# Attention values through DRAM by tokens, and the last layer's normalised input transposed by DMA

## The chip, the cores and the metric

The kernel runs on one core of a Trainium2 chip. The metric is the device time of one execution in microseconds (us). The core has five instruction streams that matter here: TensorE (PE in the profile, with its weight loads as PEld), VectorE (DVE), ScalarE (ACT), GpSimd (POOL) and SyncE (SP). SP computes nothing: every transfer of this kernel is issued from its one queue, in order, and an instruction that waits holds everything behind it.

## The reference

Input: `x` and `ctx`, each 32 batches of 128 tokens (rows) by 1024 columns. Two layers, each an attention and a feed-forward part with a residual, run over every batch independently:

```
x = x + L0_xattn(layernorm(x), ctx, ctx)   # autocorrelation by FFT, top 9 of 128 lags
x = x + L0_ffn(layernorm(x), ...)          # x @ W_base.T + mixture of 8 low-rank experts, 2 chosen
x = x + L1_xattn(layernorm(x), ctx, ...)   # attention in a window of 16
x = x + L1_ffn(layernorm(x), A, B, Wr)     # mixture of 4 low-rank experts, 2 chosen
```

The change is in the last two. In `L1_xattn` the 128 rows are channels (8 heads of 16) and the 1024 columns are the sequence:

```
q = Wq @ x + bq;  k = Wk @ ctx + bk;  v = Wv @ ctx + bv       # 128x128 by 128x1024
k, v padded with zeros: 8 columns on the left, 7 on the right
dots[h, t, w] = sum_d q[h, d, t] * k[h, d, t + w] / 4          # w = 0..15
out[h, d, t]  = sum_w softmax_w(dots)[h, t, w] * v[h, d, t + w]
x = x + Wo @ out + bo
```

In `L1_ffn` each of the 128 rows is a token of 1024 features: `logits = x @ Wr.T` (4 experts), the two largest pass a softmax, `mid = x @ A.T` (64 columns in all), each expert's 16 columns are multiplied by its gate, and the result is multiplied by `B`.

## The kernel before

**Layout.** A batch is held as two halves `g` of 128 x 512 (f32). Matrix products that need more than half precision are made of fp16 pairs: a number is split into a high and a low fp16 part (`split`), and `three` adds the products high*high, high*low, low*high in one accumulation in PSUM.

**Order.** `mk_kernel` does not emit instructions as it records them. A `Planner` notes every operation with the tiles it touches, and `plan` runs a list scheduler over the whole program: it gives every operation an estimated duration (`_cost`), a priority (batch number, length of the chain behind it, a bias by stage from `CFG`) and a tile slot, and puts it into its engine's order. `emit` then issues all of them in that order, so the order on each engine is fixed when the kernel runs, several batches are in work at a time, and every instruction comes from one line (L363 in the profile). Groups are therefore known by their tiles: `u` is one of 43 buffers of 128 x 512 f32, `d` one of 2 of twice that size, `p` a PSUM bank, `s`, `t`, `m`, `r` small tiles. `CFG` holds two phases of scheduling parameters, the second from 1459.1 on, with one bias for each stage, and a factor 1.013 on the durations of ACT, DVE and POOL.

**Stages of a batch**: `load`, `spec`, `corr`, `top`, `wt`, `inv` (layer 0's attention, for each half), `ffn0`, `gate`, `base` (its feed-forward part), then `kv`, `q`, `S`, `PV`, `wo` (layer 1's attention) and `ffn1`.

**Values before** (`attention`, L820). For each half, `three` makes `p = Wv @ ctx` (weights `wv16`, three matmuls of 512 columns), ACT adds the bias and scales it into a `u` tile, and `split` with `eng=G` makes the pair: ACT writes the high part and POOL the low part into `vpad`, a constant of 128 x 1040 x 2 fp16 whose 8 columns at each end stay zero. The product `PV` needs values by token, not by channel. So DVE transposes `vpad` in 32 x 32 blocks of 32-bit words (a word is the pair) into `d` tiles, four times a batch (L847), and SP copies them into `vbd`, a block-diagonal weight tensor of one half (128 x 32 blocks x 128 x 2 fp16), by four transfers for each half (L874). `vbd` is one buffer: the four transfers of a half can go only when the products of the half before have read it. The queries go into `qbd` in the same manner, by eight transfers for each half (L871). `S` and `PV` then run 96 matmuls of 32 columns each for a half, 48 for each quarter `qt`.

**Layer 1's feed-forward input before** (`ffn1`, L918). `ln` takes the sums of the residual, ACT squares the two halves for the variance, POOL takes the power -0.5, and `normalise` (ACT) writes the normalised half `xn`. `transposed` (L773) turns it by four TensorE transposes of 128 x 128 into a PSUM bank, ACT writes the high part from there (with the scale 32*1024) and DVE the low part (`t16`). Twelve matmuls of 68 columns for each half, with `t16` as weights and `ar4` as the moving operand, give the experts' middle columns and the logits. `ffn0` and `wt` use TensorE transposes too; they stay.

Of the kernel before, what the change touches and what calls it, by code (L numbers as in the profile page):

```python
# [14 lines left out]
F16 = mybir.dt.float16  # L15
# [12 lines left out]
TINY = 1e-30  # L28
CFG = {'nu': 43, 'nd': 2, 'en': 'G', 'cl': 'G', 'xl': 'G', 'sm': 'V', 'sw': 'A', 'wg': 'VG', 'q0': 'G', 'ns': 28, 'nt': 48, 'plan': {'phases': [{'at': 0.0, 'T': 19.88, 'margin': 178, 'win': 5, 'su': 60, 'sp': 3, 'ru': 1, 'rp': 0, 'bias': {'kv': -5.1, 'load': 10.0, 'S': -6.7, 'gate': 38.6, 'ffn1': 7.4, 'q': 0.4, 'top': 1.3, 'PV': -5.6, 'inv': 3.4, 'wt': 4.5, 'spec': 5.4, 'wo': 41.4, 'ws': -9.4, 'base': -1.7, 'ffn0': 90.1, 'corr': 5.4, 'setup': -12.6}}, {'at': 1459.1, 'T': 30.14, 'margin': 69, 'win': 6, 'su': 57, 'sp': 1, 'ru': 2, 'rp': 1, 'bias': {'kv': -32.9, 'load': -45.0, 'S': 18.4, 'gate': 125.0, 'ffn1': -67.8, 'q': 29.1, 'top': -23.6, 'PV': -37.2, 'inv': 57.1, 'wt': -20.7, 'spec': -56.0, 'wo': -29.3, 'ws': -71.2, 'base': -21.0, 'ffn0': 60.9, 'corr': -125.0, 'setup': 2.0}}], 'slack': [1.013, 0, 0]}}
NTOP = int(2 * math.log(S))  # L30
# [10 lines left out]
class _View:  # L41
# [26 lines left out]

    def windows(self, n, step, width):
        return self._step("__getitem__", (slice(None), slice(0, 1)))._wrap(n, step, width)  # L70

    def _wrap(self, n, step, width):
        f = lambda ap: bass.AP(ap.tensor, ap.offset, [list(ap.ap[0]), [step, n], [1, width]])
        return _View(self.tile, f(self.proto), self.path + ((f, None, None),))

    def resolve(self):
# [3 lines left out]
        return ap  # L80

    def region(self):

        ap = self.proto
        size = mybir.dt.size(ap.dtype)
        dims = [list(d) for d in ap.ap]
        row = dims[0][0]
        p0, f0 = divmod(ap.offset, row)
        last = f0 + sum(s * (n - 1) for s, n in dims[1:])
        return p0, p0 + dims[0][1], f0 * size, (last + 1) * size  # L90


class _Tile:
    def __init__(self, cls, slot=None, const=False):
        self.cls, self.slot, self.const = cls, slot, const
        self.log, self.users = [], {}

# [8 lines left out]
class Planner:  # L106
# [72 lines left out]
    def _cost(self, op, method, v, kw):  # L179
# [27 lines left out]
        elif eng == "DVE":  # L207
            n = max(n, size(src))
            two = method in ("tensor_copy", "tensor_scalar", "memset") and not psum and n > 64
            op.dur += 6 * n / 0.96 + 67 if method == "reciprocal" else (n * (0.5 if two else 1.0) + 64 + 59 * nsc) / 0.96  # L210
            op.dur += 70.0 * ("accum_out" in v) + {"match_replace": 67.0, "transpose": 25.0}.get(method, 0.0)
        elif eng == "Pool":
            small = mybir.dt.size(out.proto.dtype) == 2
            if method == "memset":
                op.dur += 40.0 + (0.85 if small else 0.2) * n
            else:
                rate = (2.8 if small else 1.2) if method == "tensor_scalar" else 1.88 if small else 2.1
                if any(x.proto.ap[-1][0] == 0 for x in v.values()) and n > 128:
                    rate = 1.67
                op.dur += 530.0 if kw.get("op") == ALU.pow else 150.0 + rate * n  # L220
        else:
            run = out.proto.ap[-1][1] * mybir.dt.size(out.proto.dtype)
            dram = any(x.tile is None for x in v.values())
            op.dur += (3200.0 if dram else 2900.0 if run > 128 else 3500.0) + out.shape[0] * n * mybir.dt.size(out.proto.dtype) / 360.0

            op.cold = 450.0 if dram else 720.0 if run > 128 else 840.0


# [5 lines left out]
    def plan(self, phases, slack):  # L234
# [45 lines left out]
        while events:  # L280
            now = events[0][0]
            if phases and now >= phases[0][0]:
                period, window, margin, scarce, reserve, bias = phases.pop(0)[1]
                prio = lambda o: (period * max(o.batch, 0) - o.tail - bias.get(o.stage, 0.0), o.index)
                ready = {e: sorted((prio(o), o) for _, o in l) for e, l in ready.items()}
# [80 lines left out]
def plan_args(c):  # L366
    us = lambda v: v * 1e3
    scarce = lambda f: {"u": f["su"], "p": f["sp"], "d": 9, "m": 3, "r": 9, "s": 9, "t": 9}
    reserve = lambda f: {"u": f["ru"], "p": f["rp"], "m": 1, "s": 4, "t": 6}
# [5 lines left out]
def mk_kernel(ctx: ExitStack, tc: tile.TileContext, T: dict, out: bass.AP):  # L375
# [4 lines left out]
    cp = ctx.enter_context(tc.tile_pool(name="const", bufs=1))  # L380
    pp = ctx.enter_context(tc.tile_pool(name="psum", bufs=1, space=PSUM))

    def slot(name, shape, dt=F32):
# [3 lines left out]
        "u": [slot(f"u{i}", [128, HALF]) for i in range(CFG["nu"])],  # L387
        "d": [slot(f"d{i}", [128, D]) for i in range(CFG["nd"])],
        "p": [pp.tile([128, HALF], F32, tag=f"p{i}", name=f"p{i}") for i in range(8)],
# [27 lines left out]
    def const(name, shape, dt=F32):  # L417
        return P.fixed(slot(name, shape, dt), const=True)

    def load(name, shape=None, dt=F32):  # L420
# [40 lines left out]
    k16 = keep("k16", [128, 2, D + 16], F16, 0.0)  # L461
    vpad = keep("vpad", [128, D + 16, 2], F16, 0.0)

# [19 lines left out]
    pb = B()  # L483
    PE.matmul(pb[:, 0:3], lhsT=blk1, rhs=bsum, start=True, stop=True)
    bqs, sq, bqsc, uq = (const(n, [128, 1]) for n in ("bqs", "sq", "bqsc", "uq"))
    V.tensor_scalar(bqs, pb[:, 0:1], TINY, 1.0 / W_SC, op0=ALU.add, op1=ALU.mult)
# [4 lines left out]
    V.tensor_scalar(kvs[:, 0:1], pb[:, 1:2], C_SC / W_SC, None, op0=ALU.mult)  # L491
    V.tensor_scalar(kvs[:, 1:2], rows[:, 2:3], C_SC / W_SC, None, op0=ALU.mult)
    V.tensor_scalar(kvb[:, 0:1], pb[:, 2:3], TINY, 1.0 / W_SC, op0=ALU.add, op1=ALU.mult)
    V.tensor_scalar(kvb[:, 1:2], absb[:, 2:3], TINY, 1.0 / W_SC, op0=ALU.add, op1=ALU.mult)
    V.tensor_scalar(rsx, rows[:, 1:3], 1.0 / W_SC, None, op0=ALU.mult)
    V.reciprocal(rsc, rsx)
# [133 lines left out]
    def ln(src, sums):  # L630
# [10 lines left out]
        return normalise  # L641

    def gates(vals, E, pex, tl, sc, fac, imm):

# [12 lines left out]
    def three(p, lhs, rhs):  # L657
        with P.group():
            for i, (m, r) in enumerate(THREE):
                PE.matmul(p, lhsT=lhs[:, m], rhs=rhs[:, r], start=i == 0, stop=i == 2)  # L660


# [157 lines left out]
    def attention(b, x, c16, m1, sums):  # L820
        P.stage = "kv"

        bd, skv, bsc, esc, usc, eh = s(2), s(2), s(2), s(2), s(1), s(2)
        for i in range(2):
            V.tensor_scalar(bd[:, i : i + 1], m1, kvs[:, i : i + 1], kvb[:, i : i + 1], op0=ALU.mult, op1=ALU.add)
        V.reciprocal(skv, bd)
        G.tensor_tensor(bsc, bkv_raw, skv, op=ALU.mult)
        for i in range(2):
# [4 lines left out]
        for g in range(2):  # L833
            sl = slice(8 + g * HALF, 8 + (g + 1) * HALF)
            for i, (w, hi, lo) in enumerate(((wk16, k16[:, 0, sl], k16[:, 1, sl]), (wv16, vpad[:, sl, 0], vpad[:, sl, 1]))):
                t, p = U(), B()
                three(p, w, c16[g])
                A.activation(t, p, AF.Identity, bias=bsc[:, i : i + 1], scale=esc[:, i : i + 1])
                split(hi, lo, t, G)

        words = vpad.bitcast(U32).rearrange("p n i -> p (n i)")
        v16 = []
        for g in range(2):
            t = P.tile("d")
            tv = t.bitcast(U32).rearrange("p (b c) -> p b c", c=32)
            for h in range(2):
                V.transpose(tv[:, h * 16 : (h + 1) * 16], words[:, (2 * g + h) * 256 :].windows(16, 16, 32))  # L847
            v16.append(h16(t).rearrange("p (b c i) -> p b c i", b=32, i=2))
        P.stage = "q"
# [17 lines left out]
        for g in range(2):  # L867
# [4 lines left out]
            for hp in range(4):  # L872
                hs = slice(32 * hp, 32 * hp + 32)
                SP.dma_start(out=vbd[hs, :, hs], in_=v16[g][hs])  # L874
            att = U()
# [37 lines left out]
            PE.matmul(p, lhsT=woT, rhs=att, start=True, stop=True)  # L913
            V.scalar_tensor_tensor(x[g], p, bo, x[g], op0=ALU.add, op1=ALU.add, accum_out=sums[:, g : g + 1])
        return sums


    def ffn1(b, x, sums):  # L918
        P.stage = "ffn1"
        normalise, ph = ln(x, sums), B()  # L920
        for g in range(2):
            p, t16 = transposed(normalise, g), pair(U())
            A.activation(t16[:, 0], p, AF.Copy, scale=32.0 * X_SC)
            V.scalar_tensor_tensor(t16[:, 1], p, 32.0 * X_SC, t16[:, 0], op0=ALU.mult, op1=ALU.subtract)
            with P.group():
# [79 lines left out]
def _arrays(i):  # L1005
# [10 lines left out]
            [col(a["L1_xattn_bq"]), col(a["L1_xattn_bk"]), col(a["L1_xattn_bv"]), col(a["L1_xattn_bo"])], axis=1),  # L1016
        "woT": a["L1_xattn_Wo"].T,
        "ar4T": np.concatenate([a["L1_ffn_A"].reshape(64, D), a["L1_ffn_Wr"]], axis=0).T,
# [21 lines left out]
```

## Time and profile before

| what | us |
|---|---|
| median of 3 executions | 1600.08 (1599.47 to 1602.74) |
| the profiled execution, its own time | 1600.9 |
| its span, first to last instruction | 1599.1 |
| mean granted TensorE clock | 0.974 of full |
| DVE busy | 1468.7 |
| ACT busy | 1417.8 |
| POOL busy | 1346.0 |
| transfers on SP's queue | 142.41 MB, 47.8% of the 16 DMA engines' span |

The profile page has one line of busy time for each engine over the span, the span in 40 slices, the chain of work that ended last, and groups of like instructions. A group's line reads: line, engine, operation, output tile <- input tiles, shape out <- shape in, count, then busy us and mean ns of one, then the engine's idle time before the group and what ended it. Busy time counts overlapping instructions once; the mean is that of single instructions, from start to end, and matmuls overlap, so for TensorE busy time divided by count is nearer to the price than the mean. In a timeline, start and length come first; as matmuls overlap, a group's price is the distance from its start to the next group's start.

### The profile page before, as it was taken

What the parts mean: (1) busy time and instruction counts of PE and PEld (TensorE: products, weight loads), DVE (VectorE), ACT (ScalarE), POOL (GpSimd) and SP (SyncE); (2) the same over time, 40 slices, a digit from 0 to 9 for tenths busy, and PEclk for the clock granted to TensorE, in tenths of its full rate; (3) what the DMA queues carried; (4) which work ended last, traced back from release to release, by engine and by line L of the source; (5) the groups of instructions that cost most, each with busy time, mean ns of one, the idle gap of its engine ahead of it and who ended that gap; (6) DMA issues with size and microseconds to landing.
All of it is one profiled execution on the core that took longest, in us unless ns stands there. A gap on an engine that the chain in (4) does not pass through costs nothing.

```text
span 1599.1 us, 51794 instructions
## 1 busy us (share of the span) xinstructions
PE 1520.9 (95%) x19144; PEld 1001.9 (63%) x19144; DVE 1468.7 (92%) x5042; ACT 1417.8 (89%) x2833; POOL 1346.0 (84%) x1506
## 2 busy tenths in 40 slices
PE   2599999999999999999999999999999999999985
PEld 1256666666666666666666666666666666666654
DVE  6778999999999999999999999999999999999875
ACT  4998999999999999999999999999999999999753
POOL 5789878998888899888889988888998888899742
PEclk7789999999999999999999999999999999999996
DMA  8214544554454555445455544545455454554352
GB/s 267 81 56 57 98 63 91 102 105 91 91 91 70 94 102 106 91 91 92 69 96 101 105 91 92 93 68 96 100 105 92 90 95 68 95 100 78 41 70 58
DMA packets 854620, 145.72 MB, mean 91 GB/s; under 512 B 808224, under 2 KB 810528, under 8 KB 854368
## 3 DMA queue, kind: packets, MB, share of 16 engines
q1 hardware_dynamic: 854368, 142.41, 47.8%
q8 instruction: 152, 2.49, 0.7%
q14 instruction: 100, 0.82, 0.2%
HBM read 41.80 MB, written 16.78 MB: 37 GB/s over the span
## 4 chain that ended last, share of the span: by engine, by line
PE 90%; DVE 3%; ACT 2%; issue 1%; DMA 1%; POOL 1%; SPq 1%; POOLq 0%; DVEq 0%; ACTq 0%
PE p L363 90%; ACT u L363 2%; DVE u L363 1%; POOL u L363 1%; SPq L363 1%; DVE wsp L363 0%; DVE t L363 0%; DMA cf<-in_cf 0%; DVE s L363 0%; DMA u<-u 0%; DVE wmx L363 0%; DMA vbd<-d 0%; DVE mm L363 0%; DMA qbd<-u 0%; ACT k L363 0%
## 5 line engine op out<-in xcount | busy, mean ns | idle before, releaser
L363 POOL TENSOR_TENSOR u<-u,u 128x512 f32<-128x512 f32 (+1 forms) x640 | 774.9, 1233 | 94.4 <-ACT u L363 86.8
L363 PE MATMUL p<-wsp,u 128*128 128x512 f16 (+1 forms) x2304 | 409.9, 328 | 1.8 <-DVE r L363 0.9
L363 ACT ACTIVATE u<-p 64x512 f32<-64x512 f32 (+1 forms) x576 | 331.9, 591 | 52.0 <-PE p L363 43.7
L363 ACT ACTIVATE u<-u,t 128x512 f32<-128x512 f32 (+1 forms) x448 | 320.7, 723 | 62.3 <-DVE t L363 46.6
L363 DVE SCALAR_TENSOR_TENSOR u<-p,u 128x512 f32<-128x512 f32 (+1 forms) x448 | 289.2, 681 | 54.4 <-PE p L363 27.3
L363 PEld LDWEIGHTS <-u 128*128 128x128 f16 x3072 | 218.2, 98 | 167.0 <-issue 4.2
L363 ACT ACTIVATE u<-p,t 64x512 f32<-64x512 f32 (+3 forms) x448 | 265.7, 619 | 21.1 <-PE p L363 15.0
L363 PE MATMUL p<-u,ch 128*128 128x512 f16 x960 | 239.1, 385 | 1.9 <-DVE u L363 1.9
L363 PEld LDWEIGHTS <-qbd 128*128 128x128 f16 x6144 | 172.0, 96 | 27.1 <-issue 11.1
L363 PE MATMUL p<-k,qbd 128*128 128x32 f16 x6144 | 174.6, 176 | 1.6 <-issue 1.1
L363 PEld LDWEIGHTS <-ch 128*128 128x128 f16 x960 | 95.3, 102 | 120.7 <-issue 27.3
L363 PEld LDWEIGHTS <-vbd 128*128 128x128 f16 x6144 | 164.0, 97 | 8.5 <-issue 1.4
L363 PE MATMUL p<-u,vbd 128*128 128x32 f16 x6144 | 164.4, 176 | 0.7 <-POOL u L363 0.7
L363 ACT ACTIVATE u<-u,t,t 128x512 f32<-128x512 f32 x192 | 144.0, 820 | 5.2 <-POOL t L363 5.2
L363 POOL TENSOR_TENSOR t<-t,mhalf 128x1 f32<-128x1 f32 x128 | 71.5, 558 | 79.4 <-DVE t L363 79.0
L363 POOL TENSOR_TENSOR u<-u,s 128x512 f32<-128x512 f32 x128 | 134.2, 1050 | 0.7
L363 PE MATMUL p<-u,cf 128*128 128x512 f32 x256 | 125.2, 611 | 10.0 <-POOL u L363 10.0
L363 DVE SCALAR_TENSOR_TENSOR u<-p,t,u 128x512 f16<-128x512 f32 (+1 forms) x192 | 106.0, 567 | 16.9 <-ACT u L363 8.7
L363 ACT ACTIVATE u<-u 128x512 f16<-128x512 f32 x194 | 117.3, 623 | 3.4 <-DVE u L363 3.3
L363 PE MATMUL p<-ident,u 128*128 128x128 f32 x768 | 104.4, 279 | 10.6 <-ACT u L363 10.5
L363 PEld LDWEIGHTS p<-ident,u 128*128 128x128 f32 x768 | 90.8, 144 | 22.5 <-ACT u L363 13.4
L363 ACT ACTIVATE u<-p,t,t 128x512 f32<-128x512 f32 x128 | 94.0, 775 | 0.3 <-PE p L363 0.3
(155 smaller groups left out, 2863.8 us busy)
## 6 DMA issues: line engine op xcount, KB each, us to landing
vbd<-d SPq DMA_DIRECT2D x256, 128.0 KB
u<-u SPq DMA_DIRECT2D x192, 128.0 KB
u<-in_ctx SPq DMA_DIRECT2D x64, 256.0 KB
u<-in_x SPq DMA_DIRECT2D x64, 256.0 KB
qbd<-u SPq DMA_DIRECT2D x512, 32.0 KB
out<-u SPq DMA_DIRECT2D x64, 256.0 KB
u<-u SPq DMA_DIRECT2D x64, 126.0 KB
u<-in_wbT SPq DMA_DIRECT2D x16, 256.0 KB
```

What stands on the lines that cost most here:

```text
L363: fn(*[f(a) for a in args], **{k: f(a) for k, a in kw.items()})
```

## The change

Values: `Wv @ ctx` is computed transposed, with the tokens on the rows. For each 128 tokens, the context is the weights and `wv16` the moving operand, so three matmuls of 512 columns for a half become twelve of 128. The result needs one scale for all channels, so the setup takes the largest row bound instead of one bound for each row (`gm`). The value bias is no longer added to `v`: the softmax weights sum to one, so `Wo @ bv` is added once to `bo` (`bo2`), and the padding becomes `-bv` in place of zero (`nbv`, scaled anew in every batch). ACT writes the high part and DVE the low part straight from PSUM, SP writes them to a DRAM buffer `vd` (two of them, by batch parity; 1040 rows of 256 fp16), and the four transfers into `vbd` read that buffer with a stride of one row for each window position. `vpad`, the `d` tiles and DVE's block transposes go. The planner treats a `vd` buffer as one region, so every read waits for all four writes of its batch.

Layer 1's feed-forward input: `turned` takes the place of `ln` and `transposed`. The scale 32*1024 goes into the factor and bias (two small POOL operations), ACT writes the normalised half twice, in f32 and in fp16, POOL subtracts for the low part, and SP transposes the pair of each half by one transfer in transposing mode (`turn`), 128 x 1024 fp16, from one `u` tile into another.

Planner: `nu` goes from 43 to 49 `u` tiles and `nd` goes. There is one phase instead of two, with other parameters, a bias for each stage (as before) and one for each stage and engine. `slack` goes from `[1.013, 0, 0]` to `[1.0, 0, 292.364]`: no factor on durations, 292 ns more for each transfer. Transposing transfers have a cost entry of their own. All orders and slots come out anew.

```diff
+    vd = []
+    for i in range(2):
+        vd.append(P.fixed(dp.tile([D + 16, 256], F16, tag=f"vd{i}", name=f"vd{i}")))
+        vd[i].tile.whole = True
...
+    def turned(src, sums):
+
+        nm, rs = stats(src, sums)
+        r32, nb = s(1), s(1)
+        G.tensor_scalar(r32, rs, 32.0 * X_SC, None, op0=ALU.mult)
+        G.tensor_tensor(nb, nm, r32, op=ALU.mult)
+
+        def half(g):
+            xn, t, tT = U(), pair(U()), pair(U())
+            A.activation(xn, src[g], AF.Identity, bias=nb, scale=r32)
+            A.activation(t[:, 0], src[g], AF.Identity, bias=nb, scale=r32)
+            G.tensor_tensor(t[:, 1], xn, t[:, 0], op=ALU.subtract)
+            turn(tT, t)
+            return tT
+
+        return half
...
+    def turn(dst, src):
+
+        SP.dma_start(out=dst.rearrange("p i (j n) -> p (i j) n", n=128), in_=src.rearrange("p i n -> p (i n)"), transpose=True)
...
-            for i, (w, hi, lo) in enumerate(((wk16, k16[:, 0, sl], k16[:, 1, sl]), (wv16, vpad[:, sl, 0], vpad[:, sl, 1]))):
-                t, p = U(), B()
-                three(p, w, c16[g])
-                A.activation(t, p, AF.Identity, bias=bsc[:, i : i + 1], scale=esc[:, i : i + 1])
-                split(hi, lo, t, G)
-
-        words = vpad.bitcast(U32).rearrange("p n i -> p (n i)")
-        v16 = []
-        for g in range(2):
-            t = P.tile("d")
-            tv = t.bitcast(U32).rearrange("p (b c) -> p b c", c=32)
-            for h in range(2):
-                V.transpose(tv[:, h * 16 : (h + 1) * 16], words[:, (2 * g + h) * 256 :].windows(16, 16, 32))
-            v16.append(h16(t).rearrange("p (b c i) -> p b c i", b=32, i=2))
+            t, p = U(), B()
+            three(p, wk16, c16[g])
+            A.activation(t, p, AF.Identity, bias=bsc, scale=esc[:, 0:1])
+            split(k16[:, 0, sl], k16[:, 1, sl], t, G)
+
+
+        vb = vd[b % 2]
+        t, u = M(), M()
+        pads = h16(u).rearrange("p (n r) -> p n r", r=2)
+        A.activation(t[0:16], nbv, AF.Copy, scale=skv[0:16, 1:2])
+        A.activation(pads[0:16, :, 0], nbv, AF.Copy, scale=skv[0:16, 1:2])
+        G.tensor_tensor(pads[0:16, :, 1], t[0:16], pads[0:16, :, 0], op=ALU.subtract)
+        for i in range(2):
+            SP.dma_start(out=vb[i * (D + 8) : i * (D + 8) + 8], in_=h16(u)[8 * i : 8 * i + 8])
+        for g in range(2):
+            t, p = h16(U()), B()
+            with P.group():
+                for n in range(4):
+                    for i, (m, r) in enumerate(THREE):
+                        PE.matmul(p[:, n * 128 : (n + 1) * 128], lhsT=c16[g][:, m, n * 128 : (n + 1) * 128],
+                                  rhs=wv16[:, r], start=i == 0, stop=i == 2)
+            v = t.rearrange("p (n r) -> p n r", r=2)
+            A.activation(v[:, :, 0], p, AF.Copy, scale=esc[:, 1:2])
+            V.scalar_tensor_tensor(v[:, :, 1], p, esc[:, 1:2], v[:, :, 0], op0=ALU.mult, op1=ALU.subtract)
+            SP.dma_start(out=vb[8 + g * HALF : 8 + (g + 1) * HALF].rearrange("(n p) e -> p n e", p=128),
+                         in_=t.rearrange("p (n e) -> p n e", n=4))
...
-                SP.dma_start(out=vbd[hs, :, hs], in_=v16[g][hs])
+                SP.dma_start(out=vbd[hs, :, hs].rearrange("p b n r -> p b (n r)"),
+                             in_=vb.grid(g * HALF * 256 + 64 * hp, ((256, 32), (16 * 256, 32), (1, 64))))
...
-            V.scalar_tensor_tensor(x[g], p, bo, x[g], op0=ALU.add, op1=ALU.add, accum_out=sums[:, g : g + 1])
+            V.scalar_tensor_tensor(x[g], p, bo2, x[g], op0=ALU.add, op1=ALU.add, accum_out=sums[:, g : g + 1])
...
-        normalise, ph = ln(x, sums), B()
-        for g in range(2):
-            p, t16 = transposed(normalise, g), pair(U())
-            A.activation(t16[:, 0], p, AF.Copy, scale=32.0 * X_SC)
-            V.scalar_tensor_tensor(t16[:, 1], p, 32.0 * X_SC, t16[:, 0], op0=ALU.mult, op1=ALU.subtract)
+        half, ph = turned(x, sums), B()
+        for g in range(2):
+            t16 = half(g)
```

Counted over the whole program as it is built, SP's transfers go from 38 to 44 for each batch; TensorE's instructions lose 256 transposes and gain 768 matmuls of 128 columns in place of 192 of 512.

## The prediction

> **What bounds the kernel now.** I read the busy times, then the windows by stage, then the chain that ended last, and last a timeline of TensorE.
>
> ```profile
> span 1599.1 us, 51794 instructions
> PE 1520.9 (95%) x19144; PEld 1001.9 (63%) x19144; DVE 1468.7 (92%) x5042; ACT 1417.8 (89%) x2833; POOL 1346.0 (84%) x1506
> ...
> PE 90%; DVE 3%; ACT 2%; issue 1%; DMA 1%; POOL 1%; SPq 1%; POOLq 0%; DVEq 0%; ACTq 0%
> ```
>
> ```profile
> 400.00:800.00 400.00, 400.00 (x5162) 264.81 (x5160) 383.29 (x1344) 372.34 (x751) 351.60 (x395) 1.00 0.50 90
> 800.00:1200.00 400.00, 400.00 (x5160) 265.22 (x5160) 382.65 (x1333) 372.26 (x749) 355.68 (x397) 1.00 0.51 94
> ```
>
> ```profile
> 22.27 6.07 DMA u<-u
> ...
> 217.03 1290.31 PE p L363 x16561
> 1508.05 2.73 DMA vbd<-d
> ...
> 1547.68 3.00 DMA qbd<-u
> ...
> 1554.48 2.71 DMA vbd<-d
> ```
>
> ```profile
> 440.73 0.28 PE L363 MATMUL p<-t,ones 128*128 128x2 f32 x2
> ```
>
> ```profile
> 766.92 0.28 PE L363 MATMUL p<-t,ones 128*128 128x2 f32 x2
> ```
>
> In the windows the columns are length, then busy us of PE, PEld, DVE, ACT, POOL, the granted clock, the DMA share and GB/s. The middle of the kernel is TensorE without a gap: 400 of 400 us, at clock 1.00, and one unbroken piece of 1290 us on the chain. The matmul with `ones`, one for each batch, comes back after 326.19 us for 7 batches: 46.60 us a batch. In that time DVE works 44.6 us (765.94/800), ACT 43.4, POOL 41.2. So a batch costs what TensorE needs, with the next engine 2 us below. Outside the middle lie the head (TensorE idle some 53 us of the first 200 us) and the tail (25 us idle after 1460 us).
>
> A busy TensorE need not be at its rate. The timeline gives prices from start to start:
>
> ```profile
> 1509.93 0.87 PE L363 MATMUL p<-wsp,u 128*128 128x136 f16 x12
> 1510.64 0.60 PE L363 MATMUL p<-ident,u 128*128 128x128 f32 x4
> ...
> ```
>
> ```profile
> 1542.38 1.04 PE L363 MATMUL p<-ident,u 128*128 128x128 f32 x8
> 1543.25 1.46 PE L363 MATMUL p<-u,wv 128*128 128x512 f16 x6
> 1544.55 0.54 PE L363 MATMUL p<-ar,u 128*128 128x68 f16 x12
> ```
>
> Eight transposes take 0.87 us, six value matmuls 1.30, twelve of 136 columns 0.71 (59 ns each). Pricing all matmuls of a batch like this gives 46.1 of the 46.60 us, so hardly anything but matmuls is in the period.
>
> The Trainium skill ("Trainium Kernel Development and Optimization", Best Practices) says that matmul busy time misjudges the distance to the limit, and to go by weight loads' busy share instead; that share is 66% here (264.81 of 400). Read that way, a third of TensorE would be free and taking matmuls away would gain nothing (1600). The start-to-start sum above decides against it.
>
> **The change, part by part, for one batch.**
>
> *TensorE.* Removed: 8 transposes, 0.87 us (upper bound by the group's busy time 104.4/768 = 0.136 each: 1.09). Values: 6 x 217 ns = 1.30 removed, 24 matmuls of 128 columns added. The nearest row is the 136-column one, 59 ns, by columns 56: 1.34. Bounds: the same 1.30 as before (the columns are the same), and 24 x 69 ns (busy time 52.7/768) = 1.65. Net between -0.52 and -1.09; I take -0.83. Over 32 batches -26.6 us (-17 to -35).
>
> *DVE.* Minus 4 block transposes (88.2/128 = 0.69), minus 2 low parts from PSUM (121.0/192 = 0.63), plus 2 low parts of values (like `u<-p,t,u` fp16, 47.4/64 = 0.74): -2.5, to 42.1.
> *ACT.* Minus 2 bias passes (94.0/128 = 0.73) and 2 `vpad` writes (46.4/64 = 0.73); plus 2 value passes (43.8/64 = 0.68 plus 0.15, the difference between the strided `vpad` and the plain `k` row), plus 2 pad writes (0.4 each by `m<-wqT`); two passes change from 0.55 to 0.75. Net 0.0: 43.4.
> *POOL.* Minus 2 `vpad` subtractions (81.7/64 = 1.28), plus 2 subtractions of 1.15 (295.2/256), a pad subtraction (0.24 by 36 columns to 1.15 by 512; 0.4) and one tiny operation (0.2): +0.3, to 41.5.
> All three stay under the new TensorE period of 45.8, ACT nearest (95%), so none of these is on the path; the cover is TensorE's own queue of other batches' work.
>
> *SP.* Its waits in the middle 800 us sum to 368 us, so 38 transfers cost 432/17.2 = 25.2 us a batch, 0.66 each. Six more: two pads and two value writes at 0.5 (a `ctx` load), two transposing transfers, which the trace lacks: 0.5 to 2.1 us of issue (fastest row; longest `vbd` issue 2093 ns), 0.75 taken as for a plain `u<-u` copy. That makes 28.7 of 45.8 us. The DMA engines, 50% busy for 4.45 MB a batch, get 1 MB more: 62% by bytes.
>
> *Waits.* In the new TensorE order I counted the matmul time between producer and consumer, at the prices above.
> (1) Values: 76 us lie between a half's value matmuls and its first `PV` (37 before; 38 at the least, in the first and last batches). The way is ACT 0.8, DVE 0.74, a write and a read of 0.7 + 3 each: 9 us; with 6.07 us (the slow copy in the head) for each landing 15. Hidden.
> The skill ("DMA: Bandwidth & Descriptors", Anatomy of one DMA) warns that completion can be surprisingly late where the target is HBM, about 2 us being the normal fixed part; no row here shows a waited write to DRAM. Even several times that would stay in this cover.
> (2) `vbd` is reloaded between the two halves of a batch. Cover: 8.8 us of matmuls, 11.0 before. Before, the first transfer goes 0.65 us after the last `PV`, the four issues take 2.77 to 3.45 us, the landing 2.71: 6.1 to 6.8. Margin 2.0 to 2.7 us, half of what it was. The source is now DRAM. Landing bounds 2.7 to 6.1; I take 3.0.
>
> ```profile
> 465.12 2.77 SPq L363 DMA_DIRECT2D vbd<-d  x4
> ...
> 484.98 3.45 SPq L363 DMA_DIRECT2D vbd<-d  x4
> ```
>
> (3) The turned input: from the end of the last `wo` to the first `ar` matmul TensorE has 16.8 us of other work, 9.7 before. Before, the factor is there 4.0 us after `wo` (POOL's power ends 457.6; `wo` 453.6). Now add 0.45 for two small POOL operations, 1.45 for two ACT passes, 1.15 for the subtraction, 0.75 issue, 3.0 landing: 10.8, some 2 more for queueing on ACT and POOL. Landing up to 6.1 makes 16: still just covered. Behind the two transposing transfers, which wait for POOL, SP's queue holds seven of the eight `qbd` loads of the next half, for which `S` waits 15.2 us after the half before; 8 x 0.72 + 3.0 + 2 x 0.75 = 10.3 of it is used. The value writes wait for DVE; behind them stand four spectrum copies, two outputs and the `vbd` loads of (2).
>
> *Head and tail.* The setup gains a dozen operations of 0.1 to 0.3 us and one load beside the weights' 53 us of idle TensorE. At the first `gate` matmul the new order has about 5 us less ACT and 4 us less POOL work ahead of it: -5 to 0. In the tail, after the last batch's `base`, 28.6 us of matmuls remain, 34.6 before. That part took 67.4 us (1531.7 to 1599.1) and is a chain of one batch, so 6 of the saved 26 us turn into idle time there if the chain stays as long; the turned input lengthens it by some 3, less company on DVE (28 us left, not 35.5) shortens it. Together -5 to +12, taken +3.
>
> *Sum.* Profiled execution 1600.9 - 26.6 + 3 = 1577.3; the median is 0.8 below that execution, so 1577. By the bounds: 1600 - 35 - 5 = 1560 to 1600 - 17 + 12 = 1595.
>
> **Rivals.**
> *A, slower: the `vbd` hand-over.* If the four reads from DRAM in (2) land late, or stand behind a late value write in SP's queue, TensorE stops once a batch. Free until landing is 5.0 us (margin 2.3 over 2.7), then each us costs 32; from 5.9 us it eats the whole gain. At 6.5 us: 1.5 x 32 = 48, 1577 + 48 = 1625. For: the margin halves, each run is 128 bytes, and the queue is fuller. Against: `ctx` loads from DRAM issue in 0.5 us, less than 0.69 to 0.86 for `vbd`, and before the change TensorE never stopped here in 27 batches.
> *B, the transposing transfer late.* If issue and landing exceed 3.75 by more than about 4 us in (3), `ar` stalls. At 5 more us, 1 us a batch is spilled for some batches, half of them: +16, 1593. For: no row shows this kind of transfer. Against: 7 us more cover than before.
> *C, no change.* The freed time is lost again, because ACT at 95% and POOL at 91% cannot follow a fixed order without slips of 0.8 us a batch: 1600. Against: DVE ran at 96% before without one gap on TensorE.
>
> **How the numbers follow.** Forecast 0.68 (1560 to 1595, all faster), A 0.18 (1604 to 1650), B 0.08 (1583 to 1605), C 0.06. A measurement tells 0.2% (3 us) from no change. Faster: 0.68 + 0.06 of B = 0.74. Same: C and little of B, 0.06. Slower: A and 0.02, 0.20. The range leaves out most of A: 1560 to 1604.
>
> **What would show it.** Right: the `ones` matmul returns after 45.7 to 45.9 us; TensorE is busy through the windows of the middle; `ident,u` has 512 entries, and 24 value matmuls take about 1.34 us from start to start; DVE falls by about 80 us over the span. A shows as TensorE idle before `u,vbd` once a batch, ended by the transfer `vbd<-vd`; B as idle before `ar` or `k,qbd`; C as short gaps ended by ACT or POOL. A tail over 75 us after the last `bl` matmul would break the term of +3. Wrong altogether if the period is over 46.6.

## The result and the profile after

| | before | after |
|---|---|---|
| median of 6 executions (us) | 1599.95 (1597.83 to 1602.74) | 1605.63 (1605.1 to 1606.8) |
| ratio, 95% interval | | 1.0036 (1.0023 to 1.0049) |
| span of the profiled execution | 1599.1 | 1604.9 |
| mean granted TensorE clock | 0.974 | 0.966 |

The change made the kernel slower by 0.36%, some 5.7 us. Forecast were 1577 us with a range of 1560 to 1604: the direction was wrong and the median lies just outside the range. The page of the changed kernel, its span, busy times and the chain that ended last:

```profile
span 1604.9 us, 52637 instructions
...
PE 1504.2 (94%) x19469; PEld 1005.0 (63%) x19469; DVE 1420.7 (89%) x4922; ACT 1420.5 (89%) x2833; POOL 1358.0 (85%) x1569
...
PE 52%; ACT 25%; DVE 9%; DMA 5%; issue 5%; SPq 2%; POOL 1%; ACTq 0%; POOLq 0%; DVEq 0%
```

TensorE did lose 17 us of work and DVE 48. But the chain, which ran over TensorE for 90% of the span, now does so for 52%; ACT holds 25% of it. The windows of the changed kernel (length, busy us of PE, PEld, DVE, ACT, POOL, granted clock, DMA share, GB/s) show where TensorE still has its work and where it hasn't:

```profile
400.00:800.00 400.00, 399.03 (x5245) 268.95 (x5241) 372.22 (x1322) 377.30 (x758) 359.31 (x419) 1.00 0.65 114
800.00:1200.00 400.00, 398.13 (x5294) 268.73 (x5291) 371.67 (x1317) 376.53 (x754) 360.65 (x419) 1.00 0.66 117
1520.00:1560.00 40.00, 25.13 (x474) 17.75 (x472) 22.15 (x55) 16.68 (x32) 18.55 (x25) 0.79 0.69 75
1560.00:1610.00 50.00, 19.14 (x340) 13.75 (x336) 16.32 (x51) 10.95 (x21) 10.14 (x13) 0.60 0.26 52
```

The middle is no longer without a gap: 2.8 us of idle in 800. In the timeline the period is 46.12 us, one batch from `ones` to `ones`, 0.47 less than the 46.60 before and not 0.83:

```profile
440.04 0.28 PE L364 MATMUL p<-t,ones 128*128 128x2 f32 x2
486.16 0.28 PE L364 MATMUL p<-t,ones 128*128 128x2 f32 x2
```

And the clock of the tail fell: 0.79 in the window from 1520 us, where it was 0.95 before, with TensorE busy for 25 us where it was for 33:

```profile
1520.00:1560.00 40.00, 33.24 (x542) 22.09 (x540) 30.64 (x75) 23.05 (x45) 18.62 (x25) 0.95 0.51 69
```

The `bl` matmuls come at the end of layer 0's feed-forward part, in two groups for each batch. The starts of the first group cut the span into four parts. Worked out from the two traces, in us:

| part | before | after | after minus before |
|---|---|---|---|
| start to `bl` of batch 2 | 189.7 | 195.1 | +5.4 |
| batch 2 to batch 28 | 1212.9 | 1199.0 | -13.9 |
| batch 28 to batch 31 | 127.5 | 131.0 | +3.5 |
| `bl` of batch 31 to the end | 69.0 | 79.8 | +10.8 |
| span | 1599.1 | 1604.9 | +5.8 |

So the gain is there, 13.9 us where 26 batches at the forecast 0.83 us would give 21.6, and the two ends give back 19.7 us. From the `bl` of batch 31 on TensorE is busy for 39 us (45 before), so what grew there is its idle time and not its matmuls. The experiments ask three questions: what takes 0.36 of the forecast 0.83 us a batch in the middle, what lengthened the tail, and what the head. Most of them keep the changed kernel's whole order and move, drop or double a single kind of instruction, because a new plan moves everything at once.

### The profile page after: what moved, and what is told of

Same layout as the page of the kernel before. It is cut to its first block, busy times and chain, and to the rows that moved or that the text cites. A ratio compares the mean times of both kernels' runs of the same rounds, so it can differ in the third digit from the quotient of the medians.

```text
span 1604.9 us, 52637 instructions
## 1 busy us (share of the span) xinstructions
PE 1504.2 (94%) x19469; PEld 1005.0 (63%) x19469; DVE 1420.7 (89%) x4922; ACT 1420.5 (89%) x2833; POOL 1358.0 (85%) x1569
## 4 chain that ended last, share of the span: by engine, by line
PE 52%; ACT 25%; DVE 9%; DMA 5%; issue 5%; SPq 2%; POOL 1%; ACTq 0%; POOLq 0%; DVEq 0%
PE p L364 52%; ACT u L364 24%; DVE u L364 7%; DMA vbd<-vd 3%; SPq L364 2%; DMA u<-in_x 1%; POOL u L364 1%; ACT k L364 1%; DVE t L364 1%; DMA u<-u 1%; DMA vd<-u 0%; DVE wsp L364 0%; DMA u<-in_wbT 0%; DVE wmx L364 0%; DMA u<-in_wa 0%
## 5 line engine op out<-in xcount | busy, mean ns | idle before, releaser
L364 POOL TENSOR_TENSOR u<-u,u 128x512 f16<-128x512 f32 (+1 forms) x704 | 844.6, 1227 | 56.4 <-ACT u L364 51.7
L364 PEld LDWEIGHTS <-u 128*128 128x128 f16 x3840 | 271.2, 99 | 187.7 <-DMA u<-u 13.6
L364 ACT ACTIVATE u<-p,t 64x512 f32<-64x512 f32 (+3 forms) x512 | 316.8, 648 | 22.2 <-PE p L364 12.4
L364 ACT ACTIVATE u<-p 64x512 f32<-64x512 f32 (+1 forms) x512 | 299.7, 592 | 36.9 <-PE p L364 29.7
L364 DVE SCALAR_TENSOR_TENSOR u<-p,u 128x512 f32<-128x512 f32 (+1 forms) x384 | 255.6, 678 | 30.2 <-ACT u L364 19.1
L364 DVE SCALAR_TENSOR_TENSOR u<-p,t,u 128x512 f16<-128x512 f32 (+1 forms) x256 | 157.8, 626 | 63.5 <-ACT u L364 62.7
L364 ACT ACTIVATE u<-u,t,t 128x512 f32<-128x512 f32 (+1 forms) x256 | 192.8, 829 | 4.9 <-POOL t L364 3.9
L364 POOL TENSOR_TENSOR u<-u,t 128x512 f32<-128x512 f32 x64 | 65.5, 1043 | 81.0 <-DVE t L364 78.1
L364 DVE STREAM_TRANSPOSE u<-u 128x512 f32<-128x512 f32 x128 | 89.8, 703 | 9.7 <-POOL u L364 9.2
L364 PE MATMUL p<-ident,u 128*128 128x128 f32 x512 | 82.2, 286 | 11.3 <-POOL u L364 5.4
```

Source lines behind the costliest of these rows:

```text
L364: fn(*[f(a) for a in args], **{k: f(a) for k, a in kw.items()})
```

## The experiments

### First theory of the middle: `bl` after fp16 groups

The start-to-start times after the change had one new large item: the first of three `bl` matmuls took 0.42 us in place of 0.23, twice a batch, where an fp16 group `u,ch` had been put between the two `bl` groups. The timeline of the changed kernel:

```profile
468.82 2.11 PE L364 MATMUL p<-u,ch 128*128 128x512 f16 x9
470.57 1.04 PE L364 MATMUL p<-bl,r 128*128 128x512 f32 x3
471.45 0.82 PE L364 MATMUL p<-u,ch 128*128 128x512 f16 x3
471.92 1.04 PE L364 MATMUL p<-bl,r 128*128 128x512 f32 x3
```

**joined** undoes this after planning: each of TensorE's groups between the two `bl` groups goes ahead of the first, where neither a dependence nor a tile slot stands in the way.

```diff
+            for x in pe[i + 1 : j]:
...
+                order.insert(at, order.pop(k))
```

> The changed kernel with its order kept except on TensorE: in 27 of 32 batches a group of three fp16 matmuls (u,ch) that stands between the two bl groups is put ahead of the first. Theory 1 (the new order spends part of the gain on TensorE: the first bl matmul after an fp16 group takes 0.42 us from start to start, the others 0.23, twice a batch): one of the two is saved, 0.19 us x 27 = 5.1 us, so 1600.5; the period falls from 46.13 to 45.94. Theory 2 (the 0.19 us are a wait for data and TensorE is led by the ACT, DVE and DMA part of the loop): the period stays at 46.13 and the time within 1604 to 1607.

Measured: 1607.35 us, ratio 1.0035 (1.0021 to 1.0048), the period 46.13 as before. Theory 1 fell. The timeline of this kernel says why:

```profile
470.72 1.89 PE L378 MATMUL p<-u,ch 128*128 128x512 f16 x8
472.26 1.75 PE L378 MATMUL p<-bl,r 128*128 128x512 f32 x6
473.84 0.27 PE L378 MATMUL p<-ident,m 128*128 128x128 f32 x1
```

From the first `ident,u` of the batch (450.67, and 449.64 in the changed kernel) to the `u,ch` after `ident,m` it is 23.28 us in both. The 0.19 us were never lost: the start of an f32 matmul behind an fp16 one is recorded 0.03 us after that one's start, so the fp16 matmul seems to take 0.03 and the f32 one 0.42; together 0.45, which is 0.22 + 0.23. A price from start to start holds within one form only.

### The transfers: transposing, and the `vbd` hand-over

**plain_dma** keeps every instruction and makes the transposing transfer a plain copy (the planner still books it at its old cost, so that the order stays):

```diff
+                kw = {k: v for k, v in kw.items() if k != "transpose"}
...
-        SP.dma_start(out=dst.rearrange("p i (j n) -> p (i j) n", n=128), in_=src.rearrange("p i n -> p (i n)"), transpose=True)
+        SP.dma_start(out=dst.rearrange("p i (j n) -> p (i j) n", n=128), in_=src.rearrange("p i (j n) -> p (i j) n", n=128), transpose=True)
```

The first line stands in `emit`: the instruction goes out without its transposing mode.

> The changed kernel, every instruction in its place, with the transposing transfer made a plain copy of the same tile of the same size: it leaves out the transposition. Theory 1 (the transposing transfer is hidden in the middle, and stands open only in the last batches): period 46.13 unchanged; the 10.3 us of idle before the last ar matmuls shrink by the difference of issue and landing, some 1 to 3 us, so 1602 to 1605. Rival (the transfer holds up SP's queue and the loop in every batch): the period falls by 0.2 us or more, 1599 or less.

Measured: 1605.83, ratio 1.0032 (1.0019 to 1.0044), period 46.13. In the middle the kind of transfer makes no difference. In the tail of this kernel's timeline the idle before `ar` is 9.29 us, not 10.26: the two transpositions cost the last batch 1 us. The time doesn't show this 1 us (1602 to 1605 was expected).

**half_vbd** takes half of the transfers out of the hand-over that rival A of the prediction was about:

```diff
+                if b and hp % 2:
+                    P.ops[-1].calls = []
```

> The changed kernel, every other instruction in its place, without half of the vbd reads of every batch but the first: it leaves out the values of every second pair of heads. SP loses 4 issues of 0.8 us a batch and the hand-over ends some 1.7 us sooner. Theory 3 (ACT leads): period 46.13 and 1603 to 1606. Theory 4 (the hand-over leads, or SP's queue does): the period falls to 45.7 to 45.8, 1593 to 1597.

Measured: 1605.81, 1.0028 (1.0017 to 1.004), period 46.14, DMA share down from 0.65 to 0.57. Neither the hand-over, nor SP's queue, nor the load on the DMA engines sets the period.

### The loop

The trace's one regular gap on TensorE comes once a batch, before the `ident,u` transposes of `ffn0`. TensorE's weight loads in the changed kernel show it:

```profile
495.05 0.41 PEld L364 LDWEIGHTS p<-cf,u 128*128 128x128 f32 x3 [0.24 <-issue]
495.76 0.42 PEld L364 LDWEIGHTS p<-ident,u 128*128 128x128 f32 x4 [0.29 <-ACT u L364]
```

They wait for the normalised x, which ACT makes last in a stretch without a gap. ACT in the changed kernel:

```profile
488.02 1.40 ACT L364 ACTIVATE u<-p,t 128x512 f16<-128x512 f32 x2
...
490.99 3.40 ACT L364 ACTIVATE u<-p,t 128x512 f16<-128x512 f32 x6
494.28 0.72 ACT L364 ACTIVATE u<-u,t 128x512 f16<-128x512 f32 x1
494.90 1.52 ACT L364 ACTIVATE u<-u,t,t 128x512 f32<-128x512 f32 x2
```

Does ACT lead by its load, or does TensorE? Two runs at the same order.

**one_pass** leaves out ACT's fp32 pass over ffn1's x:

```diff
             A.activation(xn, src[g], AF.Identity, bias=nb, scale=r32)
+            P.ops[-1].calls = []
...
             G.tensor_tensor(t[:, 1], xn, t[:, 0], op=ALU.subtract)
+            fn, _, kw = P.ops[-1].calls[0]
+            P.ops[-1].calls = [(fn, (t[:, 1], src[g], t[:, 0]), kw)]
```

> The changed kernel, every other instruction in its place, without the first of the two ACT passes over each half of ffn1's x: it leaves out the fp32 copy of the normalised x (POOL subtracts from x in its place), 2 x 0.75 us of ACT a batch. Theory 3 (ACT, 43.5 of 46.13 us and in a fixed order, leads the loop that TensorE now waits for once a batch): ACT falls to 42, the 0.26 us of wait before the ident,u transposes goes, the period falls to 45.7 to 45.8 (the matmuls alone) and the time by 28 x 0.36 = 10 us to 1595. Theory 4 (the vbd hand-over or another transfer leads it): period 46.13, time 1603 to 1606.

Measured: 1604.95, 1.0026 (1.0015 to 1.0037), period 46.12, although ACT fell from 43.5 to 42.3 us a batch (733.4 of 800 us). Of the freed 1.2 us, 0.9 turned into a wait of ACT for TensorE, before the pass into `r` at 474 us: 14.8 us in 16 batches, where the list of waits had none. ACT's load isn't the limit.

**less_pe** leaves out a third of the value matmuls:

```diff
+                    if n > 1:
+                        del P.ops[-1].calls[-2:]
+                        P.ops[-1].calls[-1][2]["stop"] = True
```

> The changed kernel, every other instruction in its place, with 16 of the 24 value matmuls: it leaves out the two products with a low part for half of the tokens, 8 x 0.056 = 0.45 us of TensorE a batch, half of it within the 24.1 us that the chain of waits follows on TensorE. If TensorE's rate still sets the period: 45.68 and 1605.6 - 14 = 1591. If TensorE and ACT follow one another in one loop: the period falls by the half that lies in the 24.1 us, 0.22 us, to 45.9, 1599. If ACT or a transfer leads alone: 46.13, no change.

Measured: 1601.79, 1.0005 (0.9996 to 1.0014), period 45.93 to 45.95: less by 0.19, where 0.45 us of matmuls went and 0.22 of them between `ident,u` and the end of `t,m`. The time stayed above the expected 1599. TensorE and ACT follow one another in a loop, and only work inside it counts. Read from the timeline: from `ident,u` (449.64) TensorE runs without a gap to the matmul `t,m` (37.7 us, to 487.35); DVE makes the bias of q from it; ACT starts its stretch at 488.02 and, 7.7 us later, has the normalised x; `ident,u` comes at 495.76. That is 46.12. DVE is a link of its own in this loop. Its timeline in the changed kernel:

```profile
483.99 0.75 DVE L364 SCALAR_TENSOR_TENSOR u<-p,bo,u 128x512 f32<-128x512 f32 x1
...
487.21 0.65 DVE L364 SCALAR_TENSOR_TENSOR u<-p,u 128x512 f32<-128x512 f32 x1
487.79 0.20 DVE L364 TENSOR_SCALAR t<-p,bqsc 128x1 f32<-128x1 f32 x1
```

The bias (`t<-p,bqsc`) starts as soon as DVE has finished the pass before it, some 0.3 us behind the end of `t,m`, and DVE has no gap over 0.02 us from 483.99 on, where it takes up the result of a `wo` matmul. So the loop's 4 us before ACT's stretch can also be counted over DVE; no run moved or shortened a DVE pass there.

The chain of waits did not tell this. It goes from ACT back over a transfer and another 24.1 us of TensorE:

```profile
449.64 24.10 PE p L364 x252
475.74 1.52 ACT u L364 x4
479.29 1.26 DVE u L364 x2
481.23 3.31 DMA vbd<-vd
...
489.44 1.53 ACT u L364 x4
492.77 2.94 ACT u L364 x5
```

The transfer it names was halved in half_vbd, without effect: where several releasers come close together, the one shown need not be the one that counts.

**late_load** and **double_load** test the loop inside ACT's stretch. The pass at 494.28 belongs to the `load` of a later batch and can wait. late_load moves it behind the normalisation `n` that follows it; double_load has the last line of the diff in place of the one before.

```diff
+            x = act[act.index(n) - 1]
...
+            order.insert(k, order.pop(i))
...
+            x.calls *= 2
```

> The changed kernel with its order kept, but for one ACT instruction in 28 of 32 batches: the fp16 pass over a ctx tile of a later batch, which stands right before the first ffn0 normalisation, goes behind it. Theory 5 (the period is a loop: TensorE's 37.7 us from the ident,u transposes to the matmul t,m; 0.5 us to the bias of q on DVE; 7.7 us of ACT in its order up to that normalisation; then ident,u again): the normalisation comes 0.6 us sooner, the wait of 0.26 us before ident,u goes, the period falls to TensorE's own 45.75 to 45.9, the time to 1595 to 1600. Theory 4 (another chain, over SP and the transfers, leads): 46.13, 1603 to 1607.

> The changed kernel, every instruction in its place, with that same ACT pass done twice in 28 batches (the same values are written again): 0.62 us more of ACT within the 7.7 us of the loop. Theory 5: the period rises by 0.62 us to 46.75, the time by 28 x 0.62 = 17 us to 1622. Theory 4, or TensorE alone: the period rises by at most the part not hidden, 0 to 0.2 us, 1603 to 1611.

Measured: double_load 1626.96, 1.0169 (1.0156 to 1.0182), period 46.90, or 0.77 us more in every batch, though ACT has 2.6 us a batch idle elsewhere. ACT's timeline of this run accounts for it:

```profile
1015.54 1.47 ACT L373 ACTIVATE u<-u,t 128x512 f16<-128x512 f32 x2
1016.91 1.50 ACT L373 ACTIVATE u<-u,t,t 128x512 f32<-128x512 f32 x2
```

From the first of the two passes to the normalisation it is 1.37 us, where one pass takes 0.62 (494.28 to 494.90 above): 0.75 more, not the 0.62 of the expectation. What ACT takes longer in this place, the period takes longer. That is the loop. But late_load gave 1607.61, 1.005 (1.0035 to 1.0065), period 46.15. Its ACT timeline:

```profile
495.13 0.81 ACT L378 ACTIVATE u<-u,t,t 128x512 f32<-128x512 f32 x1
495.83 0.71 ACT L378 ACTIVATE u<-u,t 128x512 f16<-128x512 f32 x1
496.45 0.81 ACT L378 ACTIVATE u<-u,t,t 128x512 f32<-128x512 f32 x1
```

and TensorE there:

```profile
496.38 0.60 PE L378 MATMUL p<-ident,u 128*128 128x128 f32 x4
496.82 0.39 PE L378 MATMUL p<-cf,u 128*128 128x128 f32 x2
497.31 0.66 PE L378 MATMUL p<-ident,u 128*128 128x128 f32 x4
```

The pass had gone between the two normalisations. The first group came early, and the second waited instead: 0.49 us from `cf,u` to `ident,u`, where 0.22 is two matmuls' time. **late_both** puts the pass behind both.

> As late_load, but the fp16 pass over a ctx tile goes behind both ffn0 normalisations of the batch (the run late_load showed the wait of 0.27 us before the second group of ident,u transposes in place of the first, the second normalisation having come no sooner). Theory 5: both normalisations come 0.6 us sooner, no wait is left before ident,u, the period falls to 45.8 to 45.9 and the time by 28 x 0.25 to 0.35 us to 1596 to 1599. If another loop of the same length stands beside this one: 46.13, 1604 to 1607.

Measured: 1601.93, 1.001 (1.0001 to 1.0019), period 45.91, no gap before `ident,u` any more. With one instruction moved, 0.22 of the missing 0.36 us a batch came back; the time is above the expected 1596 to 1599. The rest is a new wait. ACT, DVE and TensorE of this run:

```profile
494.24 1.33 ACT L378 ACTIVATE u<-u,t 128x512 f16<-128x512 f32 x2
495.47 1.06 ACT L378 ACTIVATE u<-p 128x512 f16<-128x512 f32 x2
```

```profile
496.08 1.29 DVE L378 SCALAR_TENSOR_TENSOR u<-p,u 128x512 f16<-128x512 f32 x2 [0.46 <-ACT u L378]
```

```profile
495.99 0.83 PE L378 MATMUL p<-wv,u 128*128 128x128 f16 x12
496.83 2.44 PE L378 MATMUL p<-wsp,u 128*128 128x136 f16 x28
```

In its new place the pass (the first of the two at 494.24) stands ahead of those that write the high part of ffn0's turned x (495.47); DVE's low part comes behind that, and TensorE's `wsp,u` matmuls need both. From the last `wv,u` matmul to the first `wsp,u` it is 0.06 us in every batch of the changed kernel and 0.22 in the median batch of this run: 0.16 us of wait. Without it the period is 45.75, the forecast 46.60 - 0.83 = 45.77. So, to within 0.02 us, the missing 0.36 us are waits for ACT's order, and no price of TensorE's.

### The tail

**old_tail** adds the second set of priorities, unchanged from the kernel before:

```diff
-CFG = {... 'phases': [{'at': 0.0, 'T': 20.35, ...}], ...}
+CFG = {... 'phases': [{'at': 0.0, 'T': 20.35, ...}, {'at': 1459.1, 'T': 30.14, 'margin': 69, ...}], ...}
```

> The changed kernel with the second phase of the kernel before (the set of priorities that begins at 1459.1 us) added, the first 1459 us in their old order. Theory 1 (much of the 10.8 us that the tail grew by is the order of the tail, which was planned for its own in the kernel before and is not after): the last bl matmul to the end takes about 74 us in place of 79.8 and the time is 1598 to 1601. Rival (the turned input and the DRAM round trip lengthen the last batch's chain whatever the order): 79 to 81 us, 1604 to 1607.

Measured: 1600.07, 0.9996 (0.9987 to 1.0005): as fast as before. The last part takes 72.8 us in place of 79.8. So 7 of the 10.8 us were the order, which had lost its own plan for the end.

**joined_tail** has a phase searched for this kernel with the planner's own cost table.

> The bl groups joined as in the run named joined, and a second phase of its own for the tail, searched for this kernel, from 1435.7 us on. If the bl groups (5 us) and the tail's order (8 to 9 us) add up: 1590 to 1593, faster than both kernels. If the loss lies in the mechanism and not in the order: 1600 or more.

Measured: 1598.22, 0.9981 (0.9973 to 0.999); tail 74.1 us, and the run-out of batches 28 to 31 127.7 us, 3.3 less. Joining gained nothing, so this is the tail alone. **late_load_tail** and **late_both_tail** combine the phase with the runs above:

> late_load with the second phase for the tail that the run joined_tail had (without joining the bl groups, which gained nothing). If the loop (0.25 to 0.35 us a batch) and the tail's order (5 to 7 us) add up: 1588 to 1593, faster than both kernels. If the loop is another one: 1597 to 1600, as joined_tail.

> late_both with the second phase for the tail. If the loop (7 to 10 us) and the tail's order (6 to 8 us) add up: 1588 to 1593, faster than both kernels and than joined_tail. If another loop stands beside this one: 1597 to 1599.

Measured: 1598.24, 0.9987 (0.9978 to 0.9996), no better than the tail alone, as late_load gained nothing; and 1593.72, 0.9956 (0.9944 to 0.9969): with the loop's 0.22 us the two add up.

What of the tail is the mechanism? TensorE's last batch before, in the changed kernel and in old_tail:

```profile
1580.29 1.02 PE L363 MATMUL p<-u,woT 128*128 128x512 f32 x2
1585.98 1.97 PE L363 MATMUL p<-ident,u 128*128 128x128 f32 x8 [4.66 <-ACT u L363]
1587.78 0.29 PE L363 MATMUL p<-ar,u 128*128 128x68 f16 x2
```

```profile
1581.19 2.07 PE L364 MATMUL p<-u,woT 128*128 128x512 f32 x2 [1.09 <-DVE u L364]
1593.53 0.86 PE L364 MATMUL p<-ar,u 128*128 128x68 f16 x12 [10.26 <-DMA u<-u]
```

```profile
1577.12 1.05 PE L364 MATMUL p<-u,woT 128*128 128x512 f32 x2
1588.43 0.86 PE L364 MATMUL p<-ar,u 128*128 128x68 f16 x12 [10.26 <-DMA u<-u]
```

From `wo` to `ar` it was 7.5 us before; it is 12.3 in the changed kernel and 11.3 in old_tail. So the 3.8 us by which old_tail's last part is still longer than before (72.8 against 69.0) are this way. **last_plain** turns the last batch alone on TensorE again, with a tail phase searched anew, on top of ar_later (below); `plain_turn` is `ln` and `transposed` as before the change:

```diff
-        half, ph = turned(x, sums), B()
+        half, ph = (plain_turn(x, sums) if b >= NB - 1 else turned(x, sums)), B()
```

> The kernel of ar_later with the last of the 32 batches turned by TensorE in ffn1 as in the kernel before (ln, transposed, ACT and DVE from PSUM), the other 31 by the transposing transfer, and the tail's phase searched anew (from 1415.5 us). If the turned input itself costs the tail, the way from the last wo to the first ar matmul falls from 12 to 7.5 us and the time by 2 to 5 us to 1586 to 1589. If the tail's length is the order's alone: 1590 to 1592.

Measured: 1587.15, 0.9923 (0.991 to 0.9936), the lowest median of all; its interval meets that of ar_later (0.9931 to 0.9959). Its TensorE:

```profile
1565.62 1.08 PE L383 MATMUL p<-u,woT 128*128 128x512 f32 x2
1571.36 1.82 PE L383 MATMUL p<-ident,u 128*128 128x128 f32 x8 [4.66 <-ACT u L383]
1572.97 0.32 PE L383 MATMUL p<-ar,u 128*128 128x68 f16 x2
```

7.35 us from `wo` to `ar`, as before the change (13.1 in ar_later). The turned input lengthens this way by 4 to 6 us in the one batch that has no other work beside it. How the gain over ar_later (3.5 us) divides between this and the new search wasn't tried apart.

### The head

Batch 0's `bl` comes 5.4 us earlier than before, batch 1's 5.2 us later. Between them one DVE pass over a weight takes 4.25 us. DVE of the changed kernel, then POOL and ACT:

```profile
104.24 4.25 DVE L364 SCALAR_TENSOR_TENSOR ar<-u,wsc,ar 128x256 f16<-128x256 f32 x1
```

```profile
104.51 3.70 POOL L364 TENSOR_TENSOR u<-u,u 128x512 f32<-128x512 f32 x3
```

```profile
109.92 0.72 ACT L364 ACTIVATE u<-u,t 128x512 f32<-128x512 f32 x1 [3.28 <-DVE t L364]
```

The same pass over the other half of that weight takes 0.66 us. The Trainium skill ("SBUF — State Buffer", SBUF: two separate sides) describes a port pair that VectorE, when it reads two SBUF operands, and GpSimd lock against each other for a whole instruction. The row fits in kind, and goes further: this pass ended only after the third POOL pass. **ar_only** and **ar_later** move it to just before that other half's pass, in the changed kernel and in that of late_both_tail:

```diff
+        i, k = [n for n, o in enumerate(order) if getattr(o, "low", False)]
+        order.insert(k - 1, order.pop(i))
```

> The changed kernel with its order kept, but for one DVE instruction: the pass that makes the low fp16 part of the first half of the ar weights, which takes 4.25 us at 104.2 us beside three POOL passes, goes to just before that of the second half (at about 130 us). Theory 6 (this pass, held while POOL reads SBUF, delays the head): the bias and sums behind it on DVE come 3.5 us sooner, ACT's wait of 3.3 us goes, the bl matmuls of batch 1 come 2 to 3.5 us sooner (146.5 to 148) and the time is 1602 to 1604. Rival (the head is led by ACT's own work, 23 us without a gap before batch 1's gate): less than 1 us, 1605 to 1607.

> The same move in the kernel of late_both_tail (1593.7): by theory 6 1590 to 1592, by the rival 1593 to 1595.

Measured: in ar_only's trace the pass takes 0.96 us at most, ACT's wait is gone, the `bl` of batch 1 comes at 147.8 (150.1) and the span is 1602.3. But its five times are 1604.05 to 1607.15, median 1606.17, 1.0042 (1.0028 to 1.0055): not shorter than the changed kernel's. ar_later has 1590.61, 0.9945 (0.9931 to 0.9959) against 0.9956 (0.9944 to 0.9969) without the move; the intervals overlap. That the pass is held is shown. The traces speak for a cost: the `bl` of batch 2 comes at 190.2 to 192.9 us in the three traces with the pass moved (ar_only, ar_later, last_plain) and at 194.1 to 197.3 in the 13 traces of the changed kernel and its variants without. But each trace is one execution, and the head varies by itself: without the move batch 1's `bl` comes 46.1 to 49.3 us after batch 0's. That the pass sets the head's length in most executions is not shown, and what else the head lost stays open.

## Why the prediction was wrong, step by step

**TensorE: right in price.** 24 value matmuls take 1.34 us a batch, as forecast, `ident,u` went from 768 to 512, and late_both less its one wait has the forecast period. Rivals A and B did not come: but for one wait of 0.2 us, TensorE waits for no transfer in the middle. The sign of rival C did, short gaps ended by ACT.

**"All three stay under the new TensorE period ..., so none of these is on the path": the step that failed in the middle.** The busy times were nearly right (ACT 43.5 us a batch for 43.4, DVE 42.9 for 42.1, POOL 41.5 for 41.5; over the span DVE fell by 48 us, where 80 was the sign). What failed is the inference: an engine with 2.6 us to spare in a period can still end a loop with TensorE, when its order puts the instruction that TensorE waits for behind others. That is rival C's mechanism at half its price, 0.36 us a batch for 0.8. double_load shows the loop; late_both takes 0.22 us out of it by an instruction's place and has the other 0.16 as a wait behind that same instruction.

**Waits (1) and (2): right.** half_vbd shows that the hand-over doesn't set the period, and TensorE's waits in the middle have none for the round trip through DRAM. On the chain `vbd` landed mostly in 3.3 to 3.5 us (2.8 to 4.0) where 3.0 was taken and 2.7 had been measured from SBUF. The two writes to `vd` on the chain landed in 3.3 and 3.8 us, so the late completion in DRAM that the prediction allowed for did not come in these; the section it names there is on transfers issued by GpSimd, and these are SP's.

**Wait (3): right in the middle**, though the issue was mis-sized: two transposing transfers take 3.33 us of SP's queue, 1.7 each for the 0.75 taken, and SP's waits in the 800 us leave 30 us of work a batch for the 28.7 forecast.

```profile
460.17 3.33 SPq L364 DMA_TRANSPOSE u<-u  x2
```

**Head and tail, "-5 to +12, taken +3": the term that decided.** The ends lost +5.4 (head) + 3.5 (run-out) + 10.8 (tail) = 19.7 us, where the sum lets them win 2.0 (the matmuls of 6 batches, 5.0, less the 3). The prediction counted matmuls left after the last `base` and added 3 us for the turned input. It did not price that the new plan has one phase where the old one had a second for the end, although the section on the change names it; old_tail shows that this is worth 5.6 us of time and 7.0 of the tail. And the turned input makes the way from `wo` to `ar` 4.8 us longer where nothing covers it (3.8 in old_tail), not 3. Its own sign for this term, a tail over 75 us after the last `bl` matmul, came: 78 us. It takes off -5 to 0 for the head, from work ahead of the first `gate`; batch 0 did come 5.4 us sooner, and batch 1 lost it twice over. The profiled execution missed the sum by 29 us (+5.8 for -23.6): 21.7 of them lie at the ends, 7.7 in the middle (13.9 won, where 26 batches at 0.83 make 21.6). Of the run-out's 3.5 us the searched phase took back 2.6 (37.3 to 34.7 us from batch 30 to 31). Neither half of the change was tried alone, since each would need a plan of its own.

## What to carry to other kernels

When a change comes with a new static order, price the order's ends by themselves: a batch's latency, hidden in the middle at no cost, stands open in full in the last batch, and there the old way can be kept for that batch alone. In the middle, look for loops between the busiest engine and the others rather than at busy shares; the instruction to move is the one just ahead of the one that is waited for, and what stands behind its new place has to be looked at too. Test such a loop in both directions at a fixed order, by doubling an instruction and by moving it.

## What the runs showed of the hardware

- The recorded start of an f32 matmul behind an fp16 one lies 0.03 us after the start of that one, so start-to-start times across forms are wrong by 0.19 us here while their sum is right.
- A DVE pass with two operands in SBUF was held for 4.25 us in place of 0.5 to 1.0 while three POOL passes over SBUF ran one after the other.
- Two transposing transfers of 128 x 1024 fp16 cost the last batch 1 us more than plain copies of the same tiles (10.26 us of idle for 9.29), with SP's queue busy for 2.67 us with them in place of 1.92. The Trainium skill ("Advanced Engine Details and Errata", X-Bar Transpose (TRN2)) calls the two equally fast; the runs agree to within this 1 us.
